# Five fp32 matmuls that nothing reads, behind the scores of the last two pairs of keys, in a two-layer graph network on Trainium2

## The chip, the core and the metric

The kernel runs on one core of one Trainium2 chip. A core has engines with instruction queues of their own: PE (TensorE, matrix products, with its weight loads shown apart as PEld), DVE (VectorE, elementwise work and reductions), ACT (ScalarE, activations and copies), POOL (GpSimd), and SP, which here only starts transfers. Each engine works its queue off in order and waits on semaphores that other engines raise. Matrix products land in PSUM, the accumulator memory, in banks of 512 fp32 columns for each of the 128 partitions; ACT and DVE carry the results from there to SBUF, the working memory.

The metric is device time in microseconds (us), the median over runs of the whole kernel.

## The reference, cut to what matters

There are 1250 nodes with 512 features, and 20000 edges sorted by target. Two layers are computed. The change lies in the first, in the attention over all nodes of its single graph, which turns its keys into positive features:

```
h = relu(layernorm(x))                        # 1250 x 512
# layer 1
xn = batchnorm(h);  agg = mean of xn over each node's edges;  conv = relu(agg @ W_conv + b_conv)
q, k, v = h[:256] @ Wq, h[:256] @ Wk, h[:256] @ Wv          # 8 heads of 64
def phi(t, is_query):
    t = t * 64 ** -0.25
    u = einsum('bhnd,md->bhnm', t, proj)                    # 256 random features
    diag = 0.5 * sum(t * t, -1)
    m_ = max(u, -1) if is_query else max(u, (-2, -1))
    return exp(u - diag - m_) / sqrt(256) + 1e-6
kv = einsum('bhnm,bhnd->bhmd', phi(k), v)
attn = (phi(q) @ kv) / (phi(q) . sum(phi(k)))
x = x + batchnorm(conv + attn @ Wo + h)
# layer 2
h = relu(layernorm(x));  z = (1 + eps) * h + (sum of h over each node's edges)
x = x + relu(batchnorm(relu(batchnorm(z @ W1 + b1)) @ W2 + b2))
```

For the keys, the maximum m_ is one value for each head, over all nodes and all random features, so that no exponential of a key can be taken before the scores u of all keys are there. For the queries it is one value for each node and head.

## The kernel before, in words

Nodes are handled in ten tiles of 128 rows. The program first sorts out where each target's edges lie. Then it builds, beside the attention's first half, a dense 1250 x 1250 adjacency matrix: `onehots` (line 195) lets DVE write two one-hot tables for a batch of 50 target nodes (`op` and `ok`, line 203), `count` (line 210) multiplies them on PE into a PSUM tile `acc`, ten fp16 matmuls to a batch (line 214), and ACT copies that to `adj` (line 217). There are two buffers of `op`, of `ok` and of `acc`.

Beside this runs the generator `beside` (line 289), a piece at a time. It transposes nodes, projects the keys (`features`, line 233: four blocks of four fp32 matmuls, line 242, each block copied and squared by ACT in lines 246 and 248), and then goes over eight pairs (t, b): two tiles of 128 tokens times four pairs of heads. For each pair, `scores` (line 260) takes a PSUM tile `sc` of two banks, writes the 256 scores of one head to the first half of each bank, by two matmuls of 64 rows (line 264), and hands those two halves on. ACT copies them to `kf` (line 330), and DVE takes their maxima into `kmx` (line 331). The pool of `sc` has one buffer, so the next pair's matmuls wait until both readers of the last have finished. The second half of each bank, 256 columns, is not used.

Behind the eighth pair DVE joins the maxima (`km1`, line 344), PE transposes them (line 349), DVE reduces them (line 351), PE spreads them over the partitions (line 359), and DVE works out the bias `kb` (line 362) of the sixteen exponentials that ACT takes of the keys (line 373). Meanwhile `features` does the queries, whose first block PE has multiplied before the last pairs. The queries' scores (`query`, line 456) use `scores`, and so the same buffer. From there on the kernel multiplies the normalised nodes by W_conv (`product`, line 413), finishes the attention, multiplies by the adjacency matrix (line 575), normalises, and does the second layer, most of which is matmuls (lines 707 and 764).

The order in which each engine gets its instructions is worked out when the program is built, by a list scheduler that takes what is ready first by its own model of the times. `order(...)`, a name for keep_in_program_order, pins an instruction behind the one that was written before it on the same engine. Semaphore waits are added when the program is built, too.

The tiles `ident` (a 128 x 128 identity) and `projT` (128 x 256, line 268) hold data that the kernel needs elsewhere.

Of the kernel before, what the change touches and what calls it, by code (L numbers as in the profile page):

```python
# [26 lines left out]
HEADS, DH, M = 8, 64, 256  # L27
# [42 lines left out]
def sorted_graph(ctx: ExitStack, tc: tile.TileContext, ed, x, n1g, n1b, n2g, n2b, wconv, bconv,  # L70
                 wq, wk, wv, wo, proj, eps, w1, b1, g1, be1, w2, b2, g2, be2, out):
    nc = tc.nc
# [5 lines left out]
    ident, epsc = ed.ident, ed.epsc  # L78
    order = tc.keep_in_program_order
# [146 lines left out]
    def nodes(js):  # L226
        layernorm_relu(x1, [js], lambda j: tmp.tile([S, D], F32, name="hn", tag="row"), transposed)

    def first_nodes():
        for j in range(NT):  # L230
            transposed(j, ed.x0[:, j, :])

    def features(wt, name):

        tT = ap1.tile([128, KD, TOK], F32, name=f"{name}T", tag="tT")
        dg = ap1.tile([128, NT, HEADS], F32, name=f"{name}_dg")

        pd = mm.tile([HEADS, TOK], F32, name="mm")
        for b in range(KD):
            ps = mm.tile([128, TOK], F32, name="mm")  # L240
            for k in range(KD):
                nc.tensor.matmul(ps, wt[:, k, b * 128:(b + 1) * 128], hT[:, k, :TOK],  # L242
                                 start=(k == 0), stop=(k == KD - 1))
            if b:
                nc.tensor.matmul(pd, half[b - 1], sq, start=(b == 1), stop=False)
            nc.scalar.activation(tT[:, b, :], ps, AF.Copy, scale=DH ** -0.25)
            sq = ap2.tile([128, TOK], F32, name="sq")
            nc.scalar.activation(sq, tT[:, b, :], AF.Square)
            yield
        nc.tensor.matmul(pd, half[KD - 1], sq, start=False, stop=True)  # L250
        d8 = ap2.tile([HEADS, TOK], F32, name="d8", tag="sq")
        nc.scalar.copy(d8, pd)
        yield
        ps = mm.tile([128, NT, HEADS], F32, name="mm")
        for t in range(NT):
            nc.tensor.transpose(ps[:, t, :], d8[:, t * 128:(t + 1) * 128], ident[:HEADS, :HEADS])
        nc.vector.tensor_copy(dg, ps)
        return tT, dg

    def scores(tT, t, b):  # L260

        ps = sc.tile([128, 2, 512], F32, name="sc")
        for a in range(2):
            nc.tensor.matmul(ps[:, a, :M], tT[a * 64:a * 64 + 64, b, t * 128:(t + 1) * 128],  # L264
                             projT[a * 64:a * 64 + 64, :], start=True, stop=True)
        return ps[:, :, :M]

    projT = ap1.tile([128, M], F32, name="projT")
# [9 lines left out]
    def normed(j, engine):  # L278
        n = ROWS[j]
        xn = ap2.tile([128, KD, S], F32, name="xn")  # L280
        for f in range(KD):
            src, gain, shift = hT[:, f, j * S:j * S + n], gc[:, 0, f:f + 1], gc[:, 1, f:f + 1]
            if engine is nc.scalar:
                nc.scalar.activation(xn[:, f, :n], src, AF.Identity, bias=shift, scale=gain)
            else:
                nc.vector.tensor_scalar(xn[:, f, :n], src, gain, shift, op0=ALU.mult, op1=ALU.add)
        return xn

    def beside():

        first_nodes()
        ps = mm.tile([128, M], F32, name="mm")
        for c in range(2):
            nc.tensor.transpose(ps[:, c * 128:(c + 1) * 128], pr[:, c].rearrange("p i d -> p (i d)"), ident)
        nc.scalar.copy(projT, ps)
        yield
        more = iter(range(NT, NJ))

        def node():
            for j in more:  # L300
                nodes([j])
                break

        keys = features(ed.wk, "k")
        try:
            while True:
                next(keys)
                node()
                yield
        except StopIteration as end:  # L310
            kT, kdg = end.value
        wqt = ed.wk
        nc.sync.dma_start(wqt, wq.rearrange("(k p) n -> p k n", p=128))
        ps = mm.tile([128, rows], F32, name="mm")
        nc.tensor.transpose(ps, vec, ident[:rows, :rows])
        nc.scalar.copy(vT, ps)
        nc.scalar.mul(negT, vT, -1.0)

        def stats(n):
            for f, i in itertools.islice(todo_stats, n):  # L320
                n0, w = ESPLIT[i]
                nc.vector.bn_stats(gst[:, f, i, :], hT[:, f, n0:n0 + w])

        todo_stats = iter(steps)


        for n, (t, b) in enumerate(pairs):
            ps = scores(kT, t, b)
            o = 2 * b
            nc.scalar.copy(kf[:, t, o:o + 2, :], ps)  # L330
            nc.vector.tensor_reduce(kmx[:, t, o:o + 2], ps, AX.X, ALU.max)  # L331
            if b == 0:
                pv = mm.tile([128, D], F32, name="mm")
            nc.tensor.matmul(pv, hT[:, b, t * 128:(t + 1) * 128], wvt[:, b, :], start=(b == 0), stop=(b == KD - 1))
            if b == KD - 1:
                nc.scalar.copy(va[:, t, :, :DH], pv.rearrange("p (h d) -> p h d", d=DH))
            if n < 3:
                node()
            else:
                stats(2)  # L340
            yield

        km1 = ap1.tile([128, HEADS], F32, name="km1")
        nc.vector.tensor_tensor(km1, kmx[:, 0, :], kmx[:, 1, :], ALU.max)
        queries = features(wqt, "q")
        next(queries)
        stats(len(steps))
        ps = mm.tile([HEADS, 128], F32, name="mm")
        nc.tensor.transpose(ps, km1, ident)
        km8 = ap1.tile([HEADS, 1], F32, name="km8")  # L350
        nc.vector.tensor_reduce(km8, ps, AX.X, ALU.max)
        gmv = ap1.tile([128, KD, 2], F32, name="gmv")
        for f in range(KD):
            nc.vector.bn_aggr(gmv[:, f, :], gst[:, f].rearrange("p i s -> p (i s)"))
        nc.scalar.activation(gc[:, 0, :], gmv[:, :, 1], AF.Sqrt, bias=epsc, scale=1.0)
        yield
        next(queries)
        kmall = mm.tile([128, HEADS], F32, name="mm")
        nc.tensor.matmul(kmall, km8.to_broadcast([HEADS, 128]), ident[:HEADS, :HEADS], start=True, stop=True)
        kb = ap1.tile([128, NT, HEADS], F32, name="kb")  # L360
        for t in range(NT):
            nc.vector.scalar_tensor_tensor(kb[:, t, :], kmall, -1.0, kdg[:, t, :], op0=ALU.mult, op1=ALU.subtract)
        nc.vector.reciprocal(gc[:, 0, :], gc[:, 0, :])
        nc.vector.tensor_tensor(gc[:, 0, :], gc[:, 0, :], col["n1g"], ALU.mult)
        nc.vector.tensor_tensor(gc[:, 1, :], gmv[:, :, 0], gc[:, 0, :], ALU.mult)
        nc.vector.tensor_tensor(gc[:, 1, :], col["n1b"], gc[:, 1, :], ALU.subtract)
        yield

        todo = iter([(t, o) for t in range(NT) for o in range(HEADS)])

        def exponentials(n):
            for t, o in itertools.islice(todo, n):
                nc.scalar.activation(kf[:, t, o, :], kf[:, t, o, :], AF.Exp, bias=kb[:, t, o:o + 1], scale=1.0)
                if o == HEADS - 1:
                    nc.vector.tensor_scalar(kf[:, t], kf[:, t], M ** -0.5, KEPS, op0=ALU.mult, op1=ALU.add)

        try:
            while True:
                next(queries)
                exponentials(4)  # L380
                if len(xns) < 2:
                    xns[len(xns)] = normed(len(xns), nc.vector)
                yield
        except StopIteration as end:
            qT[:] = end.value
        exponentials(NT * HEADS)

    qT = []
    rest = beside()
    nbt = N // TB  # L390
    ready = [onehots(0, (2, 3))]
# [119 lines left out]
    for f in range(KD):  # L511
        ps = mm.tile([128, TOK], F32, name="mm")
# [5 lines left out]
    for b in range(KD):  # L518
        ps = mm.tile([128, TOK], F32, name="mm")
# [45 lines left out]
    for f in range(KD):  # L565
        fs = slice(f * 128, (f + 1) * 128)
        st = tmp.tile([128, 3, 6], F32, name="st")
        for i, (n0, n) in enumerate(BSPLIT if f == KD - 1 else ESPLIT):
            c = slice(n0, n0 + n)
            ps = banks.pop(0)[:, :n] if banks else mm.tile([128, n], F32, name="mm")  # L570
            for part in (hi, lo):
                if part is lo and i == 1 and f > 0:
                    add_rows(f - 1)
                for j, k in enumerate(ROWS):
                    nc.tensor.matmul(ps, part[:k, j, fs], adj[:k, j, c],  # L575
                                     start=(part is hi and j == 0), stop=(part is lo and j == NJ - 1))
            t = p2.tile([128, n], F32, name="t", bufs=3)
            nc.vector.tensor_tensor(t, ps, rdeg[:, c], ALU.mult)

            b = at["bconv"] + f  # L580
# [39 lines left out]
    idle = mm.tile([128, 512], F32, name="mm")  # L620
# [3 lines left out]
    for g in groups:  # L624
        ps = mm.tile([S, 4, 128], F32, name="mm")
        for i, j in enumerate(g):
            n = ROWS[j]
# [48 lines left out]
    for g, after in zip(groups[2:], groups[3:] + ((),)):  # L676
# [3 lines left out]
        for j in g:  # L680
            n = ROWS[j]
# [34 lines left out]
    for t in range(6, NJ):  # L716
# [8 lines left out]
        for j in range(3 * (t - 6), min(3 * (t - 6) + 3, NJ)):  # L725
            n = ROWS[j]
# [192 lines left out]
    a, b = (Dense(ops2, m, KD // 2, o, "b2") for m in range(2))  # L919
# [735 lines left out]
```

## Time and profile before

| | us |
|---|---|
| median of three runs | 373.88 |
| lowest and highest | 373.84, 373.96 |
| the profiled execution's own time | 373.36 |
| its span, from the first to the last instruction | 371.6 |

A line of the timeline gives the start in us, the length in us, engine, source line, operation, what is written from what, the sizes, and how many instructions are merged; in brackets stand the idle time of the engine before it and what ended it. The lengths of merged PE lines overlap the next by the time that the last matmul takes to drain, so the time that one group costs is read from start to start. An fp32 matmul is two PE instructions. A line of the chain of waits gives start, length, engine, what is written, and source line, for the work that ended last.

The engines as shares of the span: PE 96%, DVE 64%, ACT 42%, POOL 9%. PE is nearly always busy from 62 us to 360 us; the stretches in which it isn't lie before and behind that.

### The profile page before, as it was taken

Reading aid. Unit: us, or ns where it says so; the run is one execution under the profiler, and the core shown is the slowest. Engines: PE = TensorE matmul, PEld = TensorE weight load, DVE = VectorE, ACT = ScalarE, POOL = GpSimd, SP = SyncE. Lnnn points to the kernel's source line nnn. Section 1 sums busy time; section 2 is a strip of 40 time slices with the busy share of each in tenths; the row PEclk is TensorE's granted clock in tenths of the full one; section 3 lists DMA queues with packets and bytes.
Section 4 is the critical chain, followed back from the end, with each engine's and each line's share of the span. In section 5 each row is a group of like instructions: output and inputs, shape, how many; then the busy total and the mean of one; then the engine's idle time right before and its main releaser. Section 6 shows DMA issues by size and latency. Waiting matters only on the chain.

```text
span 371.6 us, 4935 instructions
## 1 busy us (share of the span) xinstructions
PE 357.8 (96%) x1852; PEld 262.9 (71%) x1852; DVE 236.0 (64%) x586; ACT 156.6 (42%) x310; POOL 34.0 (9%) x49
## 2 busy tenths in 40 slices
PE   8799989999999999999999999999999999999992
PEld 5665554775656699998768888777777777777771
DVE  7999984659896235687887222182881788414673
ACT  6688459636665450111057402132652552122211
POOL 2000000000000005000000009620053000000000
PEclk9999999999999999999999999999999999999997
DMA  5953200000000571000000000150000000000124
GB/s 179 312 191 111 83 32 0 2 1 2 0 1 2 178 272 53 0 3 0 2 0 0 2 0 1 33 196 0 2 0 1 1 2 0 1 0 11 59 81 133
DMA packets 13413, 18.06 MB, mean 49 GB/s; under 512 B 1357, under 2 KB 6786, under 8 KB 13382
## 3 DMA queue, kind: packets, MB, share of 16 engines
q1 hardware_dynamic: 12670, 17.34, 14.0%
q10 hardware_dynamic: 712, 0.33, 0.3%
q8 instruction: 16, 0.26, 0.3%
q14 instruction: 15, 0.12, 0.1%
HBM read 15.11 MB, written 2.56 MB: 48 GB/s over the span
## 4 chain that ended last, share of the span: by engine, by line
PE 86%; DVE 10%; ACT 1%; issue 1%; DVEq 0%
PE mm L764 32%; PE mm L707 12%; PE mm L575 12%; PE hw L419 10%; PE mm L242 3%; PE mm L449 2%; PE mm L521 2%; DVE op L203 2%; PE mm L482 2%; PE acc L214 2%; PE sc L264 2%; PE mm L223 1%; PE mm L701 1%; DVE ok L203 1%; DVE kmx L331 1%; PE mm L472 1%
## 5 line engine op out<-in xcount | busy, mean ns | idle before, releaser
L419 PE MATMUL hw<-wconv,xn 128*128 128x512 f32 (+1 forms) x80 | 37.1, 604 | 0.3 <-ACT adj L217 0.3
L779 ACT ACTIVATE kept<-mm,vT 128x313 f32<-128x313 f32 x36 | 18.5, 520 | 42.9 <-PE mm L764 41.8
L707 PE MATMUL mm<-hi,adj 128*128 128x512 f32 (+2 forms) x100 | 32.1, 399 | 0.5 <-DVE hi L655 0.4
L707 PE MATMUL mm<-lo,adj 128*128 128x512 f32 (+2 forms) x100 | 31.7, 395 | 0.0
L131 ACT ACTIVATE r<-mv,epsc 128x1 f32<-128x1 f32 x16 | 4.7, 292 | 61.8 <-DVE mv L130 61.8
L764 PE MATMUL mm<-hid,w 128*128 128x313 f32 x96 | 25.9, 427 | 0.0
L419 PEld LDWEIGHTS hw<-wconv,xn 128*128 128x128 f32 (+1 forms) x80 | 14.1, 187 | 16.4 <-issue 14.8
L575 PE MATMUL mm<-adj,lo 128*128 128x416 f32 (+3 forms) x120 | 25.1, 355 | 0.0
L575 PE MATMUL mm<-adj,hi 128*128 128x416 f32 (+3 forms) x120 | 25.1, 355 | 0.0
L203 DVE TENSOR_TENSOR op<-iop,prow 128x1280 f16<-128x1280 f16 (+2 forms) x27 | 20.7, 766 | 6.0 <-PE acc L214 5.6
L784 DVE TENSOR_TENSOR hid<-mm,kept 128x313 f32<-128x313 f32 x24 | 10.9, 477 | 20.4 <-ACT kept L779 16.9
L764 PEld LDWEIGHTS mm<-hid,w 128*128 128x128 f32 x96 | 18.1, 190 | 6.9
L575 PEld LDWEIGHTS mm<-adj,hi 128*128 128x128 f32 x120 | 21.9, 189 | 1.1
L707 PEld LDWEIGHTS mm<-hi,adj 128*128 128x128 f32 (+2 forms) x100 | 18.4, 186 | 5.8 <-DVE hi L655 1.4
L575 PEld LDWEIGHTS mm<-adj,lo 128*128 128x128 f32 x120 | 21.8, 189 | 1.0
L698 DVE SCALAR_TENSOR_TENSOR z<-h,e,mm 128x512 f32<-128x512 f32 (+1 forms) x10 | 7.0, 746 | 23.6 <-PE mm L707 15.7
L707 PEld LDWEIGHTS mm<-lo,adj 128*128 128x128 f32 (+2 forms) x100 | 18.5, 186 | 4.6 <-DVE lo L648 0.2
L214 PEld LDWEIGHTS <-op 128*128 128x128 f16 x250 | 13.8, 97 | 7.4 <-issue 4.7
L214 PE MATMUL acc<-ok,op 128*128 128x100 f16 x250 | 16.1, 207 | 2.0 <-DVE ok L203 1.4
L702 ACT COPY zT<-mm 128x512 f32<-128x512 f32 (+1 forms) x10 | 5.3, 582 | 29.3 <-PE mm L701 29.3
L764 PE MATMUL mm<-tz,w 128*128 128x313 f32 x64 | 17.5, 426 | 0.0
L764 PE MATMUL mm<-hid,sw 128*128 128x313 f32 x64 | 17.5, 427 | 0.0
(254 smaller groups left out, 704.5 us busy)
## 6 DMA issues: line engine op xcount, KB each, us to landing
w<-in_L_gnn_W_dram SPq DMA_DIRECT2D x2, 2048.0 KB
xs<-in_x_dram SPq DMA_DIRECT2D x1, 2304.0 KB
out_dram<-xs SPq DMA_DIRECT2D x7, 256.0 KB
wk<-in_L_gnn_Wk_dram SPq DMA_DIRECT2D x1, 1024.0 KB
x<-in_x_dram SPq DMA_DIRECT2D x1, 1024.0 KB
v<-in_L_gnn_Wv_dram SPq DMA_DIRECT2D x1, 1024.0 KB
wconv<-in_L_gnn_W_conv_dram SPq DMA_DIRECT2D x1, 1024.0 KB
wk<-in_L_gnn_Wq_dram SPq DMA_DIRECT2D x1, 1024.0 KB
```

Of the source, the lines that this page charges most:

```text
L203: i = nc.vector.tensor_tensor(t[:, qs], iota.unsqueeze(1).to_broadcast(shape), keys[:, bt, qs].unsqueeze(2).to_broadcast(shape), ALU.is_equal)
L214: nc.tensor.matmul(acc[:, :, q * TG:(q + 1) * TG], op[:, q, :, i], ok[:, q, :, i].rearrange("p (j t) -> p j t", t=TG), start=(q == 0 and i ...
L242: nc.tensor.matmul(ps, wt[:, k, b * 128:(b + 1) * 128], hT[:, k, :TOK], start=(k == 0), stop=(k == KD - 1))
L264: nc.tensor.matmul(ps[:, a, :M], tT[a * 64:a * 64 + 64, b, t * 128:(t + 1) * 128], projT[a * 64:a * 64 + 64, :], start=True, stop=True)
L419: nc.tensor.matmul(ps[:n], xn[:, f, :n], wct[:, f, :], start=(f == 0), stop=(f == KD - 1))
L449: nc.tensor.matmul(ps[:, i, :], kf[:, t, hd, mb * 128:(mb + 1) * 128], va[:, t, hd, :], start=(t == 0), stop=(t == NT - 1))
L482: nc.tensor.matmul(pa[:, i, :], qfTs[n][:, i, mb, :], kv[:, mb, hd, :], start=(mb == 0), stop=(mb == 1))
L575: nc.tensor.matmul(ps, part[:k, j, fs], adj[:k, j, c], start=(part is hi and j == 0), stop=(part is lo and j == NJ - 1))
L707: nc.tensor.matmul(ps[:n], adj[:k, j, t * S:t * S + n], part[:k, j, :], start=(part is hi and j == 0), stop=(part is lo and j == NJ - 1))
L764: order(nc.tensor.matmul(banks[i], left[:, k, m * 128:(m + 1) * 128], right[:, k, i * NH:(i + 1) * NH], start=(p in (1, 2, 5) and k == 0), ...
L779: nc.scalar.activation(t[:, c, :], self.A[c], AF.Identity, bias=self.part(i, 0, c)[1], scale=1.0)
L784: order(nc.vector.tensor_tensor(self.part(i, j, c)[0], self.B[c], t[:, c, :], ALU.add))
```

## The change

`scores` gets a number `idle`. Behind its two matmuls it then issues so many more: the identity as weights, `projT` as the moving operand, 128 rows by 256 columns, fp32, into columns 256 to 511 of the tile's second bank. Nothing reads these columns. Each is pinned behind what was written before it on PE. The loop over pairs asks for two of them behind the seventh pair (n = 6) and three behind the eighth (n = 7); all other calls, the queries' among them, ask for none.

```diff
-    def scores(tT, t, b):
+    def scores(tT, t, b, idle=0):
...
         ps = sc.tile([128, 2, 512], F32, name="sc")
         for a in range(2):
             nc.tensor.matmul(ps[:, a, :M], tT[a * 64:a * 64 + 64, b, t * 128:(t + 1) * 128],
                              projT[a * 64:a * 64 + 64, :], start=True, stop=True)
+        for _ in range(idle):
+            order(nc.tensor.matmul(ps[:, 1, M:], ident, projT, start=True, stop=True))
         return ps[:, :, :M]
...
         for n, (t, b) in enumerate(pairs):
-            ps = scores(kT, t, b)
+            ps = scores(kT, t, b, {6: 2, 7: 3}.get(n, 0))
             o = 2 * b
             nc.scalar.copy(kf[:, t, o:o + 2, :], ps)
             nc.vector.tensor_reduce(kmx[:, t, o:o + 2], ps, AX.X, ALU.max)
```

## The prediction

> **What bounds the kernel now.** I read the page first, for the share of each engine and the chain that ended last.
>
> ```profile
> span 371.6 us, 4935 instructions
> ...
> PE 357.8 (96%) x1852; PEld 262.9 (71%) x1852; DVE 236.0 (64%) x586; ACT 156.6 (42%) x310; POOL 34.0 (9%) x49
> ...
> PE 86%; DVE 10%; ACT 1%; issue 1%; DVEq 0%
> ```
>
> PE sets the end for most of the span, so extra PE work costs its full length unless it falls where PE stands idle. The change sits in one stretch, so next I took the busy time in windows: from the seventh pair's scores to the queries' first scores, from there to the first product with W_conv, and the long rest. The columns are busy time (and instructions) of PE, PEld, DVE, ACT and POOL, then the granted clock.
>
> ```profile
> 45.30:50.74 5.44, 3.59 (x41) 2.43 (x41) 5.44 (x11) 3.44 (x7) 0.00 (x0) 1.00 0.35 136
> 50.74:62.30 11.56, 11.30 (x63) 6.74 (x63) 5.96 (x14) 8.53 (x20) 0.00 (x0) 1.00 0.01 1
> 62.30:357.00 294.70, 293.80 (x1415) 222.39 (x1414) 174.93 (x419) 109.78 (x206) 30.58 (x22) 1.00 0.08 28
> ```
>
> In the first window DVE never rests and PE idles 5.44 - 3.59 = 1.85 us. Behind it PE idles 0.26 us up to 62.3 us and 0.90 us in the 295 us after. Whatever delays PE at 50.74 us is therefore not made up for later. The chain of waits through this window:
>
> ```profile
> 47.26 0.68 DVE kmx L331
> 47.94 0.73 DVE op L203
> 48.67 0.59 DVE ok L203
> 49.26 0.73 DVE op L203
> 50.00 0.61 DVE kmx L331
> 50.61 0.14 issue
> 50.74 0.70 PE sc L264 x4
> 51.45 0.20 PE mm L349
> 51.65 1.73 PE mm L242 x8
> ```
>
> DVE holds it until the eighth kmx, and PE from then on: the queries' first scores wait for the one `sc` buffer. The timeline of PE shows its three pauses, 0.45, 0.62 and 0.78 us, together those 1.85 us:
>
> ```profile
> 45.30 0.70 PE L264 MATMUL sc<-projT,kT 64*128 64x256 f32 x4
> 45.94 0.70 PE L242 MATMUL mm<-hT,wk 128*128 128x256 f32 x2
> 46.48 1.07 PE L214 MATMUL acc<-ok,op 128*128 128x100 f16 x20
> 47.99 0.70 PE L264 MATMUL sc<-projT,kT 64*128 64x256 f32 x4 [0.45 <-DVE kmx L331]
> 49.32 0.65 PE L214 MATMUL acc<-ok,op 128*128 128x100 f16 x10 [0.62 <-ACT kf L330]
> 50.74 0.70 PE L264 MATMUL sc<-projT,qT 64*128 64x256 f32 x4 [0.78 <-DVE kmx L331]
> ```
>
> And that of ACT, where the two copies that read the affected tiles start 0.05 us behind the scores' last matmul (46.00 and 48.69 us):
>
> ```profile
> 46.05 0.59 ACT L330 COPY kf<-sc 128x512 f32<-128x512 f32 x1 [1.44 <-PE sc L264]
> 48.74 0.58 ACT L330 COPY kf<-sc 128x512 f32<-128x512 f32 x1 [0.56 <-PE sc L264]
> ```
>
> **Part 1, the five matmuls themselves.** The same shape stands in line 242: 128 rows, 128 columns of weights, 256 moving columns, fp32. Eight instructions, four matmuls, hold the chain for 1.73 us: 0.216 us an instruction, 0.433 us a matmul. Two cost 0.87 us, three 1.30 us, all five 2.16 us of PE. Their weight loads (187 ns for such a load in line 242) run under the matmuls, as there. The 0.33 us that the first full-height weight load loses behind the half-height scores (the gap before line 242 at 45.94 us) is paid before already, by whatever comes next; the first dummy pays it instead. It costs nothing new.
>
> **Part 2, who waits for them.** This the trace of before can't show: nothing there writes a bank while another engine waits to read it. If the copy to kf waits only for the scores, it starts as before; if it waits for the whole bank, it starts 0.87 us later at n = 6 and 1.30 us later at n = 7. What the trace has is that two readers of one `sc` tile never run together: all eight kmx start behind the end of their kf, the closest one 0.03 us behind (kf ends at 32.31 + 0.58 = 32.89, kmx starts at 32.92). That agrees with accesses to these banks being put one behind the other even without a conflict of data, though DVE was busy before most of them and its order alone could give that. I take the wait in full, and keep zero as the other end.
>
> [...]
>
> **Part 3, the chain with that wait.** Engines keep their order in this sum. Seventh pair: dummies from 45.94 to 46.81; kf starts at 46.05 + 0.87 = 46.92 and ends at 47.51. kmx started at 47.26, when DVE had just got through `xn`; the copy had been done since 46.64, so 0.62 us of the 0.87 are hidden by DVE's own work. Of the rest, 0.25 us, with a hand-over of 0.05 us as between PE and ACT, kmx is 0.30 us late. PE, which is 0.87 us late with line 242 and the twenty line-214 matmuls (their last drains at 47.55, now 48.42, and it has issued before), is no later than the buffer. The eighth scores start at 47.99 + 0.30 = 48.29. Eighth pair: kf at 48.74 + 0.30 + 1.30 = 50.34, its end at 50.92, kmx at 50.97 in place of 49.92. The delay is 1.05 us. DVE has run out of work by then (its op before kmx ends 0.30 us late, at 50.30), so it stands still for 0.6 us, and behind it in its queue wait ok, km1, xn, op. The ten line-214 matmuls sit behind the three dummies on PE and run while kf and kmx do. The queries' scores start at 50.74 + 1.05 = 51.79, and lines 349, 242, 245 and 359 follow as before, then kb and the exponentials, all 1.05 us late.
>
> Later queues: ACT's qT (line 246) stands behind kf and slips with it; the exponentials hang on line 359, so ACT's full stretch from 59 to 65 us slips as a whole. The change issues no DMA and stands behind none; SP and POOL are not touched. The sum is **+1.05 us**: 373.36 + 1.05 = 374.41 in the profiled execution's own time. The median lies 0.52 us above that execution, so 373.88 + 1.05 = **374.9 us**.
>
> **Bounds.** If no reader waits, PE alone is late: the eighth scores start when PE is free, 47.40 + 0.87 = 48.27 (47.40 is where the line-214 matmuls stop issuing, by their 46 ns spacing), 0.28 us late, and the rest fits into the pauses: +0.3 us. The same comes out if all 1.85 us of pauses take up dummies: 2.16 - 1.85 = +0.31 us. If none does and nothing overlaps, the whole 2.16 us. Below: if a new order filled every pause from 45 us on, 1.85 + 0.26 + 0.90 = 3.01 us, the kernel would gain 3.01 - 2.16 = 0.85 us.
>
> **Rivals.** *Hidden in the pauses* (+0.0 to +0.6, 374.2 us). The program's order is worked out anew with the dummies in it. DVE may take ok and the last xn before kmx instead of standing still. For it: that is 0.59 + 0.52 us of ready DVE work (ok, and two xn from start to start). Against: the queries' scores wait for kmx itself, not for what DVE does beside it, and in the trace PE does nothing of line 242's second block before the queries' scores and line 349, though its inputs were there. It also holds if readers don't wait.
>
> *A worse order* (+1.6 to +2.8, 376.1 us). An op and ok pair slips ahead of the eighth kmx: 0.73 + 0.59 = 1.32 us, and 1.05 + 1.32 less the 0.6 us that DVE stood still is +1.8; with the seventh also missed, more. For it: at both kmx DVE's queue already has such work in front while the copy is done (0.62 and 0.60 us of it). Against: the wait is longer now, so ready work fits before it.
>
> *Faster.* The order changes so that PE gets work of its own into its pauses, line 242's second block (1.73 us) foremost: it has to fill more than 2.16 of the 3.01 us to gain anything, and all to reach 0.85 us, 373.0 us. Against: 1.16 of the 3.01 us lie far from the edit. A better clock can't be what is gained in this execution: the granted clock is 1.00 in all three windows, and line 242 issues each 0.216 us behind the pauses as before them. Could the timed runs hold a slow stretch that the profile lacks? The median is 0.52 us above, so no more than that is there to win, and 1.05 - 0.52 is still a loss.
>
> That the matmuls are dropped as unread is excluded by line 1523: seven such matmuls stand in the trace.
>
> **How the numbers follow.** What this kernel's measurement can tell from no change I take as 0.2%, 0.75 us: 373.13 to 374.63. Forecast (+0.7 to +1.6) 0.53; hidden 0.25; worse order 0.12; an order that gains 0.10. Slower gets most of the forecast and the worse order: 0.62. Same gets the hidden case, the rim of the forecast and a small part of the last: 0.29. Faster keeps 0.09. The forecast's own range is 374.6 to 375.5; the whole range, 374.0 to 375.8, leaves out most of the faster case and the far half of the worse order.
>
> **What would show it.** In the profile after: ten PE instructions of `sc` from projT and ident, 0.216 us apart; kf behind them, near 46.9 and 50.3 us; the eighth kmx near 51.0; the queries' scores near 51.8 us; line 764's long stretch shifted by the same. If kf starts while dummies run, Part 2 is wrong. If the second block of line 242 comes before the queries' scores, the order has changed and the hidden or the faster case holds. If line 242 issues faster than each 0.216 us, or the median moves while the span doesn't, I have misjudged the clock.

## The result, and the profile after

| | before | after |
|---|---|---|
| median, us (executions) | 373.88 (5) | 375.81 (5) |
| lowest and highest | 373.26, 374.19 | 375.29, 376.09 |
| ratio, 95% interval | | 1.0054, 1.0042 to 1.0066 |
| the profiled execution, its span | 373.36, 371.6 | 375.79, 374.0 |

The change costs 1.93 us by these medians; 1.05 us were forecast. Over all executions of the study the difference is smaller: 129 of the kernel before have a median of 374.10 us, 17 of the changed kernel one of 375.79 us, 1.69 us more.

The page's head and the engines' shares of the chain that ended last, after:

```profile
span 374.0 us, 4955 instructions
...
PE 360.2 (96%) x1862; PEld 264.9 (71%) x1862; DVE 234.6 (63%) x586; ACT 156.7 (42%) x310; POOL 34.3 (9%) x49
...
PE 85%; DVE 10%; ACT 2%; DMA 1%; issue 1%; SPq 1%; DVEq 0%; ACTq 0%
```

There are ten more PE instructions, five matmuls of two each. Below, the same three windows as before: from the seventh pair's scores to the queries' first scores, from there to the same product with W_conv at which the second window ended before, and the long rest.

```profile
45.65:52.70 7.05, 5.75 (x51) 4.32 (x51) 6.04 (x13) 3.51 (x7) 0.00 (x0) 1.00 0.36 137
52.70:64.27 11.57, 11.31 (x64) 6.74 (x64) 5.46 (x12) 8.54 (x20) 0.00 (x0) 1.00 0.00 0
64.27:359.00 294.73, 293.83 (x1415) 222.42 (x1414) 173.43 (x419) 109.82 (x206) 30.84 (x22) 1.00 0.09 28
```

The first window grew from 5.44 to 7.05 us, by 1.61 us; the other two are as before, to 0.03 us where they end at the same instruction (the second: 11.56 and 11.57 us). In it PE is busy 2.16 us longer, exactly the five matmuls, and idle 1.30 us instead of 1.85: of 1.85 us of pauses only 0.55 took up dummies. That is the whole effect. The rest of the 2.4 us between the two spans lies outside: the seventh scores start 0.35 us later (45.65 against 45.30), before any dummy, and the tail behind the adjacency product is 0.45 us longer. A second profile of the changed kernel (below) has +0.87 and +0.82 us in these places, and two kernels without dummies (mm3_none_again and late, below) differ there by 0.7 and 1.0 us, so I take these parts for chance. From here on I give one measure that is free of them: **from the seventh pair's scores to the first product with the adjacency matrix** (line 575, now 578), "the stretch". Before it took 87.76 us, after 89.36: **+1.60 us**.

The timeline of PE in the first window:

```profile
45.65 0.70 PE L265 MATMUL sc<-projT,kT 64*128 64x256 f32 x4
46.28 1.13 PE L268 MATMUL sc<-projT,ident 128*128 128x256 f32 x4
47.25 0.59 PE L242 MATMUL mm<-hT,wk 128*128 128x256 f32 x2
47.69 1.02 PE L214 MATMUL acc<-ok,op 128*128 128x100 f16 x19
48.85 0.70 PE L265 MATMUL sc<-projT,kT 64*128 64x256 f32 x4
49.48 1.56 PE L268 MATMUL sc<-projT,ident 128*128 128x256 f32 x6
50.88 0.66 PE L214 MATMUL acc<-ok,op 128*128 128x100 f16 x11
52.70 0.70 PE L265 MATMUL sc<-projT,qT 64*128 64x256 f32 x4 [1.16 <-DVE kmx L334]
```

Line 268 is the dummies: 0.97 us from start to start for two, 1.40 us for three. The pause ahead of the eighth scores has gone, the one ahead of the queries' scores has grown from 0.78 to 1.16 us. The two copies on ACT, and DVE around the seventh and the eighth kmx:

```profile
47.45 0.59 ACT L333 COPY kf<-sc 128x512 f32<-128x512 f32 x1 [2.49 <-PE sc L268]
...
51.09 0.59 ACT L333 COPY kf<-sc 128x512 f32<-128x512 f32 x1 [0.65 <-PE acc L214]
```

```profile
46.83 1.37 DVE L289 TENSOR_SCALAR xn<-hT,gc 128x128 f32<-128x128 f32 x5
48.12 0.68 DVE L334 TENSOR_REDUCE kmx<-sc 128x2 f32<-128x512 f32 x1
48.72 0.81 DVE L203 TENSOR_TENSOR op<-iop,prow 128x1280 f16<-128x1280 f16 x1
49.45 0.67 DVE L203 TENSOR_TENSOR ok<-iok,kcol 128x1000 f16<-128x1000 int16 x1
51.13 0.83 DVE L203 TENSOR_TENSOR op<-iop,prow 128x1280 f16<-128x1280 f16 x1 [1.01 <-PE acc L214]
51.87 0.69 DVE L334 TENSOR_REDUCE kmx<-sc 128x2 f32<-128x512 f32 x1
```

kf waits for the last dummy, 0.20 us behind the time at which PE goes on to other work (47.25 and 50.88 us). The second kf is put down to line 214, which ended at about the same moment; it starts 0.21 us behind the dummies, as the first does. And an op stands in front of the eighth kmx, as before, but now it has to wait for a line-214 matmul itself. Ahead of the seventh kmx stand five pieces of xn, where the kernel before has three; they let it start at 48.12 us, 0.08 us behind the end of kf.

### The profile page after: what moved, and what is told of

It reads as the page before. It is cut to its first block, busy times and chain, and to the rows that moved or that the text cites. A ratio compares the mean times of both kernels' runs of the same rounds, so it can differ in the third digit from the quotient of the medians.

```text
span 374.0 us, 4955 instructions
## 1 busy us (share of the span) xinstructions
PE 360.2 (96%) x1862; PEld 264.9 (71%) x1862; DVE 234.6 (63%) x586; ACT 156.7 (42%) x310; POOL 34.3 (9%) x49
## 4 chain that ended last, share of the span: by engine, by line
PE 85%; DVE 10%; ACT 2%; DMA 1%; issue 1%; SPq 1%; DVEq 0%; ACTq 0%
PE mm L767 31%; PE mm L710 12%; PE mm L578 12%; PE hw L422 10%; PE mm L242 3%; PE mm L452 2%; PE mm L524 2%; PE sc L265 2%; PE mm L485 2%; PE acc L214 2%; DVE op L203 2%; PE mm L223 1%; PE mm L704 1%; PE mm L475 1%; DVE kmx L334 1%; DVE ok L203 1%
```

## The experiments

No kernel here leaves work out. Times are medians of so many executions, against the kernel before on the same chip; "busy" and "idle" are PE's in the stretch, and what a kernel's stretch costs over its control is what PE does more, less what it idles less.

| kernel | stretch | busy | idle | time (n) | ratio, 95% interval |
|---|---|---|---|---|---|
| before | 87.76 | 85.63 | 2.13 | 374.10 (129) | |
| after | 89.36 | 87.78 | 1.58 | 375.81 (5) | 1.0054 [1.0042, 1.0066] |
| again | 89.37 | | | 375.56 (12) | 1.0018 [1.0000, 1.0036] |
| six | 88.26 | 86.57 | 1.69 | 375.01 (12) | 1.0015 [0.9992, 1.0038] |
| seven | 88.41 | 87.14 | 1.27 | 374.73 (12) | 0.9999 [0.9984, 1.0015] |
| one_each | 88.40 | 86.83 | 1.57 | 374.69 (12) | 1.0004 [0.9986, 1.0022] |
| one_each_pin | 88.92 | 86.73 | 2.19 | 375.79 (4) | 1.0053 [1.0032, 1.0074] |
| after_pin | 89.69 | 87.86 | 1.83 | 376.04 (6) | 1.0052 [1.0035, 1.0069] |
| mm3_none | 89.39, clock halved for a while | | | 374.87 (10) | 1.0004 [0.9976, 1.0031] |
| mm3_none_again | 87.84 | 85.44 | 2.40 | 373.84 (10) | 1.0010 [0.9991, 1.0029] |
| mm3_same | 89.44 | 87.60 | 1.84 | 375.28 (10) | 1.0039 [1.0012, 1.0066] |
| mm3_own | 87.85 | 87.38 | 0.47 | 373.66 (10) | 0.9990 [0.9968, 1.0012] |
| own_more | 88.38 | 88.07 | 0.31 | 375.05 (10) | 1.0017 [0.9995, 1.0039] |
| copies | 91.18, clock halved for a while | | | 378.04 (8) | 1.0104 [1.0070, 1.0139] |
| two_none | 91.65 | 90.14 | 1.51 | 375.53 (10) | 1.0037 [1.0007, 1.0067] |
| two_same | 93.30 | 91.79 | 1.51 | 377.27 (4) | 1.0104 [1.0059, 1.0150] |
| late | 87.83 | 85.44 | 2.39 | 374.80 (10) | 1.0027 [1.0000, 1.0054] |
| after_late | 89.44 | 87.62 | 1.82 | 375.20 (10) | 1.0036 [1.0013, 1.0059] |
| swap | 86.41 | 86.13 | 0.28 | 372.61 (10) | 0.9962 [0.9936, 0.9988] |
| after_swap | 88.25 | 88.19 | 0.06 | 374.24 (10) | 1.0013 [0.9990, 1.0036] |

The theory first held was: the copy to kf waits for the whole bank, dummies included, and through kf and kmx PE's next scores come late (theory 1). Its rival was that PE's own 2.16 us make the price, wherever the matmuls write (theory 2).

**The changed kernel once more** (again), to see what is chance.

> The changed kernel once more, for the spread between executions. Of the 2.4 us by which the span of its first profile is longer, 1.61 us arise between the seventh pair's scores and the queries' first scores (7.05 us there, 5.44 us before), 0.35 us earlier and 0.44 us in the last stores. Theory 1 (the readers' wait): the 7.05 us come again within 0.05 us, and the 0.35 and 0.44 us are chance and come out otherwise. Theory 3 (a part of the loss is a fixed one outside that stretch): the same 0.35 and 0.44 us again. Median 375.3 to 376.1 by both.

The stretch repeats to 0.01 us; the time differs by 0.25 us from the first comparison. A profiled stretch tells tenths of a microsecond, these medians don't.

**One part alone** (six, seven, one_each). The edit is the table of counts, {6: 2} in six, {7: 3} in seven, {6: 1, 7: 1} in one_each:

```diff
-            ps = scores(kT, t, b, {6: 2, 7: 3}.get(n, 0))
+            ps = scores(kT, t, b, {6: 2}.get(n, 0))
```

> Two dummies behind the seventh pair alone. Theory 1: the copy to kf comes 1.05 us later, of which DVE's own queue covers 0.62; kmx and all behind it 0.5 us late; the stretch takes 5.9 to 6.0 us, the median is 374.4. Theory 2 (PE is the bound, and each dummy costs its PE time whatever waits): 0.97 us, stretch 6.4 us, median 374.85.

> Three dummies behind the eighth pair alone. Theory 1: kf 1.49 us later, 0.60 us of it covered by DVE's queue, so 0.9 us, and up to 0.2 us more if a one-hot table is late in front of kmx: stretch 6.3 to 6.6 us, median 374.8 to 375.0. Theory 2: 1.40 us, stretch 6.85 us, median 375.3.

> One dummy behind each of the two pairs. Theory 1: each makes its kf about 0.6 us later, which is just what DVE's queue covers (0.62 and 0.60 us): stretch 5.4 to 5.6 us, median 373.9 to 374.05, though PE works 0.9 to 1.0 us more. Theory 2: 0.9 to 1.0 us, stretch 6.35 us, median 374.85.

Two behind the seventh scores cost 0.50 us of the stretch, three behind the eighth 0.65, one behind each 0.64. The expectations count only up to the queries' first scores, 5.44 us before; there the three kernels take 5.95, 6.45 and 6.45 us. six and seven are what theory 1 has for them. one_each is a plain miss for theory 1 as a sum over one chain (5.4 to 5.6 us) and close to its rival (6.35 us). In this measure the parts nearly add up, 0.51 and 1.01 us against 1.61 us for both. In the stretch they don't, 1.15 against 1.60 us: seven and one_each have 40 line-214 matmuls ahead of the queries' first scores, where before, after and six have 30, and some 0.36 us of their delay come back behind these scores. Why one_each is late there, DVE's order shows:

```profile
47.81 0.68 DVE L334 TENSOR_REDUCE kmx<-sc 128x2 f32<-128x512 f32 x1
48.41 0.81 DVE L203 TENSOR_TENSOR op<-iop,prow 128x1280 f16<-128x1280 f16 x1
49.15 0.67 DVE L203 TENSOR_TENSOR ok<-iok,kcol 128x1000 f16<-128x1000 int16 x1
49.74 0.82 DVE L203 TENSOR_TENSOR op<-iop,prow 128x1280 f16<-128x1280 f16 x1
50.47 0.67 DVE L203 TENSOR_TENSOR ok<-iok,kcol 128x1000 f16<-128x1000 int16 x1
51.06 0.68 DVE L334 TENSOR_REDUCE kmx<-sc 128x2 f32<-128x512 f32 x1
```

There are two op and ok pairs between the two kmx, where the kernel before has one and a half, and the second kmx starts 0.45 us behind the end of its kf (50.61 us). The first starts 0.50 us behind the end of its own (47.31 us), since five pieces of xn stand ahead of it, too. seven has two pairs and two xn, and its eighth kmx starts 0.20 us behind kf. Each edit is also a new order. In one_each this is the rival called a worse order, in another kernel than the one that was forecast.

**Who waits: the same five matmuls in the readers' bank and in a bank of their own.** A buffer fewer for `mm` makes room; mm3_none is the control without dummies, mm3_same has the change as it is, and mm3_own all of this:

```diff
-    mm = att.enter_context(tc.tile_pool(name="mm", bufs=4, space=PSUM))
+    mm = att.enter_context(tc.tile_pool(name="mm", bufs=3, space=PSUM))
+    ownp = att.enter_context(tc.tile_pool(name="own", bufs=1, space=PSUM))
+    own = ownp.tile([128, 256], F32, name="own")
...
-            order(nc.tensor.matmul(ps[:, 1, M:], ident, projT, start=True, stop=True))
+            order(nc.tensor.matmul(own, ident, projT, start=True, stop=True))
```

> The kernel before with three buffers instead of four in the mm pool, no dummies: the control for the next two, which need a bank of their own. The measure is the time from the seventh pair's scores to the first product with the adjacency matrix, which no disturbance at the start or the end of the span touches: 87.76 us in the kernel before, 89.36 and 89.37 us in two profiles of the changed one. Expected here by all theories: as before or up to 1.5 us longer.

> The changed kernel with three mm buffers: dummies in the scores' second bank as in the change. Both theories: 1.3 to 1.9 us longer in that measure than the control without dummies.

> The same five dummies at the same places, but into a bank of their own that nobody reads. Theory 1 (the copy to kf waits for the whole bank): the copy starts 0.05 us behind the scores' last matmul again, while dummies still run; the dummies fall into PE's pauses, and the measure is 0.0 to 0.6 us above the control. Theory 2 (PE is the bound and the dummies cost their PE time whatever waits): 1.3 to 1.9 us above the control, as with the shared bank.

> The kernel with three mm buffers and no dummies, once more: it is the control for the kernel whose dummies write a bank of their own, and its first profile had a spell of a lower clock between 50 and 56 us. Theory A (PE's clock is lowered by chance behind the thin stretch around 45 to 51 us, and a third mm buffer costs nothing): if this profile has no such spell, the stretch from the seventh scores to the adjacency product takes 87.8 to 87.9 us; with the spell 89.3 us or so, and of the ten or so timed executions several have a mean clock at or below 0.989. Theory B (the three buffers themselves cost 1.6 us): 89.3 us with a clock of 1.00 in every window.

The first profile of the control fell into a spell of half clock (last section), so it was run again: 87.84 us, the third buffer had cost nothing. In the shared bank the dummies add 1.60 us to that, in a bank of their own 0.01 us. The medians of these two kernels, taken on one chip, are 375.28 and 373.66 us, 1.62 us apart. The dummies of mm3_own, on PE, and its copies, on ACT:

```profile
47.10 1.13 PE L270 MATMUL own<-projT,ident 128*128 128x256 f32 x4
...
49.80 1.56 PE L270 MATMUL own<-projT,ident 128*128 128x256 f32 x6
```

```profile
47.25 0.58 ACT L335 COPY kf<-sc 128x512 f32<-128x512 f32 x1 [1.46 <-PE sc L267]
49.94 0.58 ACT L335 COPY kf<-sc 128x512 f32<-128x512 f32 x1 [2.11 <-PE sc L267]
```

The copies are released by the scores (line 267) and start while the dummies run. The windows from the seventh scores to the first product with W_conv (1.3 us ahead of the end of the second window above), of mm3_none_again, mm3_same and mm3_own:

```profile
44.79:60.54 15.75, 13.60 (x100) 8.65 (x99) 10.16 (x23) 10.70 (x24) 0.00 (x0) 1.00 0.13 47
```

```profile
45.38:62.74 17.36, 15.77 (x111) 10.55 (x110) 10.26 (x23) 10.78 (x24) 0.00 (x0) 1.00 0.14 52
```

```profile
46.47:62.24 15.77, 15.55 (x110) 10.49 (x110) 10.29 (x22) 10.95 (x25) 0.00 (x0) 1.00 0.15 59
```

PE is busy 13.60, 15.77 and 15.55 us. With the dummies in a bank of their own nearly all of them fall into its pauses (0.22 us of idle time are left); in the readers' bank the pauses stay, since the dummies delay what PE is waiting for. Theory 2 falls, and so does the view that unused columns are free. Two reserves. The order differs, too: mm3_own has the queries' first scores at the end of the window, and no op in front of the eighth kmx. And the dummies are in another tile as well as in another bank. The wait is a semaphore that is added when the program is built; whether it is put there for the tile or for the bank, and whether the chip would need it, no run here tells.

**More dummies, own bank** (own_more, three and four).

> Seven dummies, three and four, into a bank of their own that nobody reads (three mm buffers). With five (two and three) the stretch from the seventh scores to the adjacency product took 87.85 us, 2 of 10 executions had a mean clock at or below 0.989. Theory 1 (dummies cost only through the readers of a shared bank, and PE's own time for them falls into its pauses as long as there are pauses): the two further ones are 0.87 us of PE where 1.85 us of pauses were and 2.16 are already spent, so 0.3 to 0.9 us of them show: 88.2 to 88.7 us; kf still starts about 0.05 us behind the scores. Theory A of the clock (PE work in the thin stretch keeps the clock up): no execution at or below 0.989. Its rival (the spells come by chance, whatever is in the stretch): about 2 of 10 again.

Once the pauses are full, the rest shows: two more matmuls, 0.87 us, add 0.53 us, with 0.06 us of idle time left in the window. The expectation on the clock missed: no execution was to have a mean clock of 0.989 or less, and 4 of 10 had (last section).

**Late readers without PE work** (copies). ACT copies the scores twice and three times more, into a tile that nothing reads, ahead of kf. PE does nothing more.

```diff
+            for i in range({6: 2, 7: 3}.get(n, 0)):
+                nc.scalar.copy(junk[:, i % 2], ps)
-            nc.scalar.copy(kf[:, t, o:o + 2, :], ps)
+            i = nc.scalar.copy(kf[:, t, o:o + 2, :], ps)
+            if n >= 6:
+                order(i)
```

> No dummies on PE. In their place ACT copies the scores two times more behind the seventh pair's and three times more behind the eighth pair's, into a tile that nothing reads, ahead of the copy to kf, so that kf is done 0.95 and 1.45 us later. Theory 1: late readers cost by themselves, 0.8 to 1.6 us in the measure, with no PE work added. Theory 2: PE has the same work, so 0 to 0.2 us.

The timeline of PE, from the seventh scores to the eighth:

```profile
45.39 0.70 PE L264 MATMUL sc<-projT,kT 64*128 64x256 f32 x4
46.02 0.70 PE L242 MATMUL mm<-hT,wk 128*128 128x256 f32 x2
46.56 1.07 PE L214 MATMUL acc<-ok,op 128*128 128x100 f16 x20
49.16 0.70 PE L264 MATMUL sc<-projT,kT 64*128 64x256 f32 x4 [1.53 <-DVE kmx L336]
```

The eighth scores come 3.77 us behind the seventh instead of 2.69, and PE waits 1.53 us for kmx instead of 0.45: late readers make PE late, with no PE work added. Not all of it is the copies: they make kf end 0.97 us later (at 47.70 us), and an op stands in front of kmx besides and holds it until 48.34 us. The stretch is 3.42 us longer, where 0.8 to 1.6 us were expected; neither that nor the 1.04% of the whole time is the price of late readers alone. The order has twenty line-214 matmuls more ahead of the queries' first scores, the last ten of which wait for an adj copy, and all eight executions had a mean clock of 0.989 or less (last section).

**The op in front of kmx** (after_pin, one_each_pin): the op of batch 13 is pinned behind the eighth kmx on DVE.

```diff
+    behind = {13: 7}
...
+                if bt in behind:
+                    tc.add_manual_dep(i.ins, last_kmx[behind[bt]].ins.name, mybir.DependencyInfo(
+                        mybir.DependencyClass.NoSync, mybir.DependencyReason.DATA), reason="order")
```

> The changed kernel, with one more hand-written order: the one-hot table of batch 13 (op, line 203) stands behind the eighth kmx in DVE's queue, not in front of it. Measured from the seventh pair's scores to the first product with the adjacency matrix: before 87.76 us, after 89.36. Theory 1 (the readers wait for the whole bank; of the 1.60 us, 0.19 come from the op that waits for the last line-214 matmul in front of the eighth kmx): the eighth kmx starts right behind kf, 0.15 to 0.19 us earlier, and the stretch takes 89.2 us. Rival (that op fills time in which kmx has to wait anyway, or what it gives comes back later): 89.3 to 89.4 us, no change.

> One dummy behind the seventh and one behind the eighth scores, with the one-hot table of batch 13 pinned behind the eighth kmx. Without the pin the two dummies cost 0.64 us (88.40 us against 87.76). Theory 1 (with so short a wait DVE's queue covers most of it; what cost 0.64 us was the new order on DVE, which put an op and an ok in front of the eighth kmx): the eighth kmx starts at the end of its kf, and the stretch takes 87.8 to 88.1 us. Rival (the price goes by the number of dummies, or the new order costs in another place): 88.3 to 88.5 us again.

In after_pin the eighth kmx starts right behind kf:

```profile
51.65 0.69 DVE L340 TENSOR_REDUCE kmx<-sc 128x2 f32<-128x512 f32 x1 [1.58 <-ACT kf L339]
52.25 0.82 DVE L206 TENSOR_TENSOR op<-iop,prow 128x1280 f16<-128x1280 f16 x1
52.98 0.16 DVE L353 TENSOR_TENSOR km<-kmx 128x8 f32<-128x8 f32 x1
```

That is 6.06 us behind the seventh scores instead of 6.22, as expected, and the queries' first scores come 0.25 us earlier. But the op now stands in front of km1, and ACT does three exponentials instead of two ahead of an adj copy that the product with W_conv waits for: the stretch is 0.33 us longer, not shorter. one_each_pin is the same, 0.41 us gained at the queries' scores and 0.52 us lost in the stretch. So op's share in the delay is shown at the queries' scores; that the stretch would gain by it was wrong, in both.

**Through what the late readers make PE late.** Two buffers for the scores should cut the link from kmx to the next scores (two_none without dummies, two_same with them).

```diff
-    mm = att.enter_context(tc.tile_pool(name="mm", bufs=4, space=PSUM))
-    sc = att.enter_context(tc.tile_pool(name="scores", bufs=1, space=PSUM))
+    mm = att.enter_context(tc.tile_pool(name="mm", bufs=2, space=PSUM))
+    sc = att.enter_context(tc.tile_pool(name="scores", bufs=2, space=PSUM))
```

> The kernel before with two buffers for the scores (two banks each) and, to make room, two mm buffers instead of four. No dummies. Measured from the seventh pair's scores to the first product with the adjacency matrix (87.76 us with one buffer). Theory 1 (in this stretch PE waits for the one scores buffer to be read): the pauses of PE ahead of the eighth scores and of the queries' first scores, 0.45 and 0.78 us, are gone; two mm buffers may cost as much elsewhere, so the stretch is left open, 86.5 to 90 us. It is the control for the next kernel.

> The same with the five dummies behind the seventh and eighth scores, in the same unused columns. Theory 1 (a dummy makes the reader late, and the late reader makes PE late only through the one scores buffer): with a second buffer PE goes on to other work while kf and kmx wait, and the five dummies cost 0.0 to 0.9 us of this stretch against the kernel with two buffers and without them, half of the 1.60 us or less. Rival (the late maxima cost the time through km1, the bias and the exponentials, or PE's own 2.16 us do, so that the number of buffers makes no difference): 1.4 to 2.2 us more.

The price stays, 1.65 us, but this doesn't tell what it should. The window up to the product with W_conv, without and with the dummies:

```profile
43.15:60.78 17.63, 17.63 (x121) 11.33 (x120) 14.60 (x37) 12.89 (x29) 0.00 (x0) 1.00 0.21 60
```

```profile
43.14:62.41 19.27, 19.27 (x131) 12.87 (x129) 14.24 (x37) 12.89 (x29) 0.00 (x0) 1.00 0.15 55
```

The control has no pause left in which a dummy could hide, so there it is PE's own time that shows. That it is 1.65 us and not the full 2.16 fits the queries' first scores, though no run tests it: in the control their two halves stand apart and hold PE for 0.62 and 0.63 us (from 59.00 and 60.15 us), with the dummies they stand together and hold it for 0.63 us in all (from 61.78 us). The next two keep one buffer and put the queries' first scores behind the queries' second block of line 242 on PE, so that they no longer stand first in PE's queue behind the eighth pair:

```diff
+            if late:
+                tc.add_manual_dep(i.ins, late.ins.name, mybir.DependencyInfo(
+                    mybir.DependencyClass.NoSync, mybir.DependencyReason.DATA), reason="order")
...
-        ps = scores(qT, t, b)
+        ps = scores(qT, t, b, marks["q", 1] if n == 0 else None)
```

> The kernel before with one hand-written order: the queries' first scores stand behind the queries' second block of line 242 on PE, so that they no longer stand first in PE's queue behind the eighth pair. Now the transposes of km1 (line 349 of before) are next, and they wait for km1 instead of the buffer. Control for the next kernel; the stretch from the seventh scores to the adjacency product takes 87.2 to 88.2 us (87.76 before): what PE waits for is 0.2 us later, and it has one thing less to do until then.

> The same order with the five dummies in the scores' columns. Against the control: if the price of the dummies goes through the one scores buffer to the queries' first scores (the forecast's chain), it falls to 0.9 us or less. If it goes through the maxima, whatever reads them first (km1 and its transposes here), it stays at 1.4 to 1.8 us.

87.83 and 89.44 us: 1.61 us again, with the forecast's last link taken out. PE in late, behind the eighth scores:

```profile
49.52 0.63 PE L214 MATMUL acc<-ok,op 128*128 128x100 f16 x10 [0.62 <-ACT kf L335]
51.44 0.26 PE L214 MATMUL acc<-ok,op 128*128 128x100 f16 x2 [1.29 <-DVE ok L203]
51.54 0.27 PE L354 MATMUL mm<-ident,km 128*8 128x128 f32 x1
```

What is next on PE waits for DVE all the same, for an ok that stands behind the eighth kmx and for km1 behind that; in after_late this pause is 1.65 us. So the buffer isn't the only link. In this order, too, what PE needs next comes through DVE's queue behind the eighth kmx.

**PE work of its own in the pauses** (swap, after_swap). The queries' second block is written ahead of the transposes of km1, and these and the queries' first scores are pinned behind it.

```diff
         next(queries)
         stats(len(steps))
+        next(queries)
         ps = mm.tile([HEADS, 128], F32, name="mm")
-        nc.tensor.transpose(ps, km1, ident)
+        i = nc.tensor.transpose(ps, km1, ident)
+        tc.add_manual_dep(i.ins, marks["q", 1].ins.name, mybir.DependencyInfo(
+            mybir.DependencyClass.NoSync, mybir.DependencyReason.DATA), reason="order")
...
         yield
-        next(queries)
         kmall = mm.tile([128, HEADS], F32, name="mm")
```

> The kernel before with the queries' second block written ahead of the transposes of km1, and these and the queries' first scores pinned behind it on PE: 1.73 us of PE work that waits for nothing comes between the seventh and the eighth scores. If the pauses of this stretch (1.85 us) are what there is to win, the block fills the one of 0.45 us and most of the others: 86.2 to 87.2 us for the stretch, 372.5 to 373.3 us in all. If what waits is only moved on (the maxima are as late as before or later, and ACT with them), 87.5 to 88.5 us.

> The same with the five dummies. Theory 1, now as a rule for the price: PE's 2.16 us, less what of PE's pauses in the stretch they take up, and the pauses that stay are those in which PE waits for the readers, which the dummies make late. With fewer pauses in the control there is less to take up: 1.6 to 2.2 us more than the kernel without them. Rival (the price is the readers' delay alone, and PE has other work to do meanwhile here): 0.9 us or less.

PE in swap:

```profile
46.85 0.70 PE L266 MATMUL sc<-projT,kT 64*128 64x256 f32 x4
47.49 2.00 PE L244 MATMUL mm<-hT,wk 128*128 128x256 f32 x8
49.54 0.70 PE L266 MATMUL sc<-projT,kT 64*128 64x256 f32 x4
50.18 0.70 PE L244 MATMUL mm<-hT,wk 128*128 128x256 f32 x2
50.72 1.07 PE L214 MATMUL acc<-ok,op 128*128 128x100 f16 x20
51.82 1.03 PE L247 MATMUL mm<-sq,half 128*8 128x256 f32 x4
```

Eight instructions of the queries' blocks (line 244), where there were two, stand between the two pairs of scores, and no pause is left. The stretch takes 86.41 us, 1.35 us less than before, and this kernel beats both: 372.61 us, ratio 0.9962 [0.9936, 0.9988]. With the five dummies in the shared bank the stretch is 1.84 us longer: with next to no pauses (0.28 us of idle time) they cost most of their length.

## Why the forecast was right in kind and too small

**The bounds and the mechanism (Part 2) held.** The readers wait for the dummies in full, kf starts 0.20 us behind the group; mm3_same against mm3_own puts a number to the lower bound that was kept beside it: 0.01 us if they don't, where some 0.3 were reckoned. In the forecast's sum the wait in full was my estimate, which no row of before shows; the waits in these traces look like a guard for the whole bank, though one for the whole tile would look the same.

**The dummies' length (Part 1) held for PE, not for the reader.** 2.16 us of PE were forecast and 2.16 measured. But the step that says of the gap behind the half-height scores that the first dummy pays it instead and "it costs nothing new" failed. Nothing new for PE; but now it lies ahead of the reader. The group took 0.97 and 1.40 us from start to start, where 0.87 and 1.30 were taken (line 242 behind it got the 0.10 us back: 0.44 us for two instructions instead of 0.54), and kf starts 0.20 us behind the group, where it had started 0.11 us behind the scores' 0.64. So kf is 1.05 us late in the seventh pair, not 0.87, and in the eighth by a further 1.49, not 1.30.

**The cover by DVE's own work (Part 3) held, in the seventh pair with some luck.** 0.62 us were to be hidden there; kmx came 0.51 us late, which is 1.05 - 0.62 and the 0.08 us behind the end of kf. But two more pieces of xn, 0.5 us of DVE work, had moved ahead of this kmx, and they happened to be done just then. Without a late kf they would have made it about as late by themselves, as they do in one_each, so of this half microsecond it isn't shown that the copy alone made it. In the eighth pair, too, kmx as after_pin has it, right behind kf, is 1.44 us late: 0.51 + 1.49 - 0.56 (before, kmx started 0.60 us behind the end of kf, here just behind it).

**"Engines keep their order in this sum" failed by two xn and one matmul.** The xn cost next to nothing here, 0.03 us beyond the forecast's hand-over of 0.05. The last of the twenty line-214 matmuls of two batches moved behind the eighth scores and the three dummies (19 and 11 in place of 20 and 10), and the op ahead of the eighth kmx waited for it until 51.13 us. The forecast let that op end 0.30 us late and go unnoticed. It adds 0.16 us to kmx (6.22 against 6.06 us in after_pin).

So the sum, each term as measured: 0.18 (longer and later-draining group, seventh) + 0.19 (the same, eighth) + 0.16 (op) on 1.05 is 1.58 us, against 1.60 measured. The mechanism was right; mis-sized were the delay of the two copies, 1.05 and 1.49 us instead of 0.87 and 1.30, and the op, taken at nothing. Together they make the price half as large again as the forecast. What is left to 1.93 us of the first medians lies outside the stretch.

**The chain's last link was named too narrowly.** The forecast hung everything on the one buffer; late and after_late show the same price without that link.

**The rivals.** Hidden in the pauses is what happens in a bank of its own, and not in this one. A worse order is what happened to one_each, up to the queries' first scores. Faster by a new order was the right idea for another edit: swap fills the pauses with PE work that waits for nothing. The clock, argued away for the profiled execution, did play a part in others, below. One reading was wrong without a consequence: line 1523 stands in the trace with eleven such matmuls, not seven.

## What to carry to other kernels

Work in an engine's pause is free only if what ends the pause doesn't wait for it: five matmuls cost 1.60 us in the bank whose reader PE was waiting for, and 0.01 us in another. Price such an edit from the reader's side, with the group's first-instruction loss and drain in it (0.10 us, and 0.20 us from the group to the copy), and expect of each pinned or added instruction a new order around it: three small edits here that were priced along one chain (one_each, after_pin, one_each_pin) missed by half a microsecond or more. If an engine idles for a late reader, look first for work of its own that is ready: that was worth 1.35 us of the stretch here.

## What was not expected of the hardware

PE's granted clock falls to 0.50 for some 3.4 us in some executions. The profiles of the kernels before and after show it at the end of the span, where PE is done: from 366.7 us before, 1.4 us behind PE's last matmul, and from 371.0 us after, 3.8 us behind it. Five profiles show a spell of it elsewhere (mm3_none, copies, mm3_own, own_more and swap), each behind 3.41 us, about as long as a spell, in which PE is busy for 1.3 to 2.0 us, without a pause of more than 1.53 us. The first profile of mm3_none shows it; the windows are the 3.41 us around the pauses, and three microseconds behind them:

```profile
47.50:50.91 3.41, 1.55 (x17) 0.99 (x18) 3.41 (x6) 2.47 (x6) 0.00 (x0) 0.95 0.03 12
51.00:54.00 3.00, 3.00 (x10) 1.99 (x10) 2.88 (x8) 0.00 (x0) 0.00 (x0) 0.50 0.03 5
```

```profile
50.73 1.22 PE L264 MATMUL sc<-projT,qT 64*128 64x256 f32 x4 [0.79 <-DVE kmx L331]
51.89 0.37 PE L349 MATMUL mm<-ident,km 128*8 128x128 f32 x1
52.06 2.86 PE L242 MATMUL mm<-hT,wk 128*128 128x256 f32 x8
```

PE is busy 1.55 us of 3.41, its longest pause is 0.79 us, and then the clock is 0.50 and line 242 takes 2.86 us instead of 1.89. By windows of 1 us the clock is 0.80, 0.50, 0.50, 0.50 and 0.99 from 50 us on: 1.71 us of clock are lost, or 3.4 us at half. It costs 1.55 us of the stretch (89.39 against 87.84). The profile of copies has the same from 53 us on, and those of mm3_own, own_more and swap have it once between 12 and 18 us, long before the seventh scores; here mm3_own:

```profile
12.00:16.00 4.00, 3.12 (x15) 2.73 (x16) 3.65 (x9) 0.97 (x3) 0.00 (x0) 0.57 0.93 297
```

Of the kernel before, 21 of 129 executions had a mean clock of 0.989 or less and a median of 376.04 us, the others 374.00. Of the changed kernel's 17 executions none had. Its least busy 3.41 us here hold 2.25 us of PE work, those of the kernel before 1.56. That the dummies, beside their price, take such spells away fits these counts, but isn't shown: at the rate of the kernel before, 17 executions without one would come up once in some twenty times by chance. Against it stands own_more, where no 3.41 us around the former pauses hold less than 3.35 us of PE work: it had 4 in 10. The mean clock doesn't say where a spell lies, and it misses some: in the profiled executions of mm3_own, own_more and swap, with the spells between 12 and 18 us, it is 0.992 or 0.993. after_late holds 1.76 us and had none in 10, six 2.00 us and had 3 in 12, and the profile of late holds 1.33 us and shows no spell behind them. What sets off a spell, no run here tells. The spells may be one reason why the medians differ by more or less than the stretch from one comparison to the next.
